# Adapter numbers read from DRAM into registers, and block 0's B and A sent on two queues behind the first piece of x

## The chip, the cores and the metric

The kernel runs on one core of a Trainium2 chip. The metric is the device time of that core in microseconds (us), and the figure for a kernel is the median of its runs.

## What is computed

x holds 8 sequences of 256 tokens with 1024 features, 2048 tokens in all. Each sequence has an adapter number between 3 and 7 that picks one of 8 pairs of low-rank matrices A (1024 x 16) and B (16 x 1024). The adapter's output goes through a feed-forward layer with 2752 hidden features whose inputs are rounded to FP8, and x is added at the end. In the reference, cut to what matters:

```python
def _L0_cond_ref(x, A, B, adapter_ids):
    B_sel = B[adapter_ids]
    A_sel = A[adapter_ids]
    Bx = jnp.einsum('bni,bri->bnr', x, B_sel)
    out = jnp.einsum('bnr,bor->bno', Bx, A_sel)
    return out * SCALING          # 1.0

def _fake_quant_fp8_linear(x, w_q, in_scale, w_scale):
    x_q = jnp.clip(x / in_scale, -_FP8_MAX, _FP8_MAX)
    x_dq = x_q.astype(jnp.float8_e4m3fn).astype(jnp.float32) * in_scale
    return jnp.einsum('bsh,ih->bsi', x_dq, w_q * w_scale)

gate_out = _fake_quant_fp8_linear(y, gate_w, gate_in_scale, gate_w_scale)
up_out = _fake_quant_fp8_linear(y, up_w, up_in_scale, up_w_scale)
hidden = jax.nn.silu(gate_out) * up_out
x = x + _fake_quant_fp8_linear(hidden, down_w, down_in_scale, down_w_scale)
```

## The kernel before

Everything is transposed: features lie on the 128 partitions, tokens along the rows. The 2048 tokens form four blocks t = 0 to 3 of 512, each of two sequences; the 1024 features form eight groups k of 128. The hidden features form 22 chunks c, 21 of 128 and a tail of 64. Weights lie in DRAM as float32, and TensorE reads the upper half of each word as bfloat16.

**The stages on TensorE (PE).** Every matmul goes through one helper at line 470, which holds PE to the order of the program. PE starts with 16 matmuls on a tile of zeros (`warm`, line 634), which need no data. Then it computes B times x for block 0 (`bx`, line 635, in the order of k, with 4 more matmuls on zeros after k = 3), 7 more matmuls on zeros, A times that (`c`, line 637), and then gate and up of chunk 0 for block 0 (`y`, line 638). ScalarE (ACT) and VectorE (DVE) round `c` to FP8 as `xg`. `turns=(2, 2, 2, 2)` at line 638 makes the first eight of chunk 0's sixteen matmuls read only the first half of its weights. Chunks 1 to 4 follow for block 0; in the middle of chunk 4 comes `bx` of block 1 (line 642), then the same five chunks for block 1, with B and A of blocks 2 and 3 among them, and so on; chunks 5 to 21 run over all four blocks; the down projection (`yd`) ends the kernel. After each gate and up, ACT applies Silu and DVE multiplies (lines 609 and 610).

**The loads, in the order of the program, lines 394 to 420.** x of block 0 comes in three pieces: k = 0 to 3 (1 MB), k = 4 to 6 (768 KB), k = 7 (256 KB). Below they are called x0, x4 and x7 after `load_x(0, 0)`, `load_x(0, 4)` and `load_x(0, 7)`. Gate and up weights of one chunk are 1 MB; chunk 0 comes in two halves (c0a, c0b), the others whole (c1 to c4). A load of B for one sequence is 68 KB in 128 rows (it also brings the six scales), one of A for block 0 or 1 is two transfers of 16 rows, 32 KB each. Nearly all are issued by SyncE's queue (SP); the adapter numbers and the B of sequence 0 are issued by ACT's.

**The adapter numbers.** Line 306 brings the eight numbers to SBUF (`ids_i`); `adapter_of` (line 363) loads one of them from SBUF into a register of the queue that asks, and checks its range. `load_b` (line 366), `load_a_two` (line 373) and line 420 use the register as an offset into DRAM. SP reads number 1 ahead of B of sequence 1 (line 396), number 0 between its A loads (line 402), and numbers 2 to 7 in a row (line 406), behind the loads of c0 to c4 and ahead of B and x of block 1.

**The limit on transfers in flight.** The framework gives the transfers of SP and ACT eight semaphores in turn, so a transfer is issued only when the one eight places before it has landed. SP carries out its queue in order; a wait at one transfer holds up all behind it.

**The tail of the down weights.** `wt` (line 656) is one transfer of 512 KB. The program has it near the end of the chunks; the framework's order puts it on SP's queue behind the A loads of blocks 2 and 3.

## Time and profile before

| | |
|---|---|
| median of 3 runs | 476.85 us (476.83 to 477.06) |
| time of the profiled execution | 477.12 us |
| its span, first to last instruction | 475.3 us |
| outside the span | 1.8 us |
| granted TensorE clock | 1.000 |
| PE busy | 469.8 us, 99% of the span, 2514 matmuls |
| ACT busy / DVE busy | 192.5 us / 105.6 us |
| read from HBM / written | 44.60 MB / 8.39 MB |
| waits of PE for a transfer, all before 17.3 us | 4, together 1.45 us |

All moments below are microseconds from the start of the span. A line such as `PE y L470 <- DMA w_gu<-w_gu` reads: the matmuls at line 470 that write `y` waited for the transfer from `w_gu` in DRAM to the tile `w_gu`. SPq and ACTq are the queues' own instructions: an issue of a transfer is a `DMA_DIRECT2D`, and the load of a register is a `TENSOR_LOAD`. "To landing" is the time from the start of an issue until all 16 parts of the transfer are down.

### The profile page before, as it was taken

What the parts mean: (1) busy time and instruction counts of PE and PEld (TensorE: products, weight loads), DVE (VectorE), ACT (ScalarE), POOL (GpSimd) and SP (SyncE); (2) the same over time, 40 slices, a digit from 0 to 9 for tenths busy, and PEclk for the clock granted to TensorE, in tenths of its full rate; (3) what the DMA queues carried; (4) which work ended last, traced back from release to release, by engine and by line L of the source; (5) the groups of instructions that cost most, each with busy time, mean ns of one, the idle gap of its engine ahead of it and who ended that gap; (6) DMA issues with size and microseconds to landing.
All of it is one profiled execution on the core that took longest, in us unless ns stands there. A gap on an engine that the chain in (4) does not pass through costs nothing.

```text
span 475.3 us, 6009 instructions
## 1 busy us (share of the span) xinstructions
PE 469.8 (99%) x2514; PEld 217.0 (46%) x2514; DVE 105.6 (22%) x163; ACT 192.5 (40%) x249; POOL 1.0 (0%) x7
## 2 busy tenths in 40 slices
PE   8999999999999999999999999999999999999997
PEld 4454544444444444444444444444444444444444
DVE  1333432121212222121212212132120121031031
ACT  1322447995556654533454554359212022021000
POOL 0000000000000000000000000000000000000000
PEclk9999999999999999999999999999999999999999
DMA  8995013422222112222211111123335255063031
GB/s 291 406 405 186 1 48 133 176 88 90 88 88 89 24 66 89 90 88 88 90 30 60 44 62 56 61 83 123 103 146 161 64 185 161 22 213 114 3 116 66
DMA packets 13780, 53.44 MB, mean 112 GB/s; under 512 B 1650, under 2 KB 2930, under 8 KB 10674
## 3 DMA queue, kind: packets, MB, share of 16 engines
q1 hardware_dynamic: 13600, 52.92, 32.1%
q8 instruction: 21, 0.34, 0.3%
q14 instruction: 13, 0.11, 0.1%
q10 hardware_dynamic: 146, 0.07, 0.0%
HBM read 44.60 MB, written 8.39 MB: 111 GB/s over the span
## 4 chain that ended last, share of the span: by engine, by line
PE 96%; DMA 3%; SPq 0%; issue 0%; DVE 0%
PE y L470 62%; PE yd L470 31%; DMA w_gu<-w_gu 2%; PE c L470 1%; PE bx L470 1%; DMA x<-x 1%; DMA ids_i<-ids 0%; SPq L363 0%; SPq L366 0%; DVE o L695 0%; PE count L470 0%
## 5 line engine op out<-in xcount | busy, mean ns | idle before, releaser
L470 PE MATMUL y<-xg,w_gu 128*128 128x512 fp8e4 x1376 | 298.4, 379 | 0.9 <-DMA w_gu<-w_gu 0.9
L470 PEld LDWEIGHTS <-w_gu 128*128 128x128 bf16 x1376 | 134.0, 98 | 163.8 <-DMA w_gu<-w_gu 1.8
L470 PE MATMUL yd<-hid,w_d 128*128 128x512 fp8e4 (+2 forms) x693 | 146.0, 373 | 0.0
L609 ACT ACTIVATE g<-y,gate_s 128x512 f32<-128x512 f32 (+1 forms) x88 | 59.8, 681 | 137.2 <-PE y L470 137.2
L610 DVE SCALAR_TENSOR_TENSOR hid<-y,up_by_down,g 128x512 fp8e4<-128x512 f32 x84 | 63.1, 751 | 220.3 <-PE y L470 162.2
L470 PEld LDWEIGHTS <-w_d 128*128 128x128 bf16 x693 | 66.6, 98 | 79.0 <-issue 1.7
L456 ACT ACTIVATE junk<-w_d 128x1408 bf16<-128x1408 uint16 (+1 forms) x16 | 21.2, 1324 | 88.4 <-DMA w_d<-w_d 88.3
L695 DVE SCALAR_TENSOR_TENSOR o<-yd,down_s,x 128x512 f32<-128x512 f32 x28 | 20.0, 748 | 107.4 <-PE yd L470 92.8
L456 ACT ACTIVATE junk<-w_gu 128x2048 bf16<-128x2048 uint16 (+1 forms) x22 | 41.0, 1863 | 0.0
L463 ACT ACTIVATE junk<-hid 128x2048 bf16<-128x2048 fp8e4 x21 | 40.0, 1905 | 0.4
L463 ACT ACTIVATE junk<-xg 128x2048 bf16<-128x2048 fp8e4 x8 | 15.3, 1909 | 0.3
L528 ACT ACTIVATE xg<-c,inv 128x512 fp8e4<-128x512 f32 x16 | 9.7, 688 | 8.6 <-PE c L470 8.6
L526 DVE TENSOR_SCALAR xg<-c,inv 128x512 fp8e4<-128x512 f32 x16 | 10.9, 744 | 2.8 <-PE c L470 2.8
L470 PE MATMUL warm<-zeros 128*128 128x512 bf16 (+1 forms) x27 | 6.5, 402 | 1.2 <-DVE zeros L309 1.2
L695 DVE SCALAR_TENSOR_TENSOR o<-yd,down_s,xg 128x512 f32<-128x512 f32 (+2 forms) x5 | 3.2, 644 | 12.3 <-PE yd L470 12.3
L516 ACT COPY bm<-bx 64x128 f32<-64x128 f32 x4 | 1.0, 262 | 9.7 <-PE bx L470 9.6
L470 PE MATMUL bx<-x,b 128*32 128x128 f32 x128 | 4.3, 276 | 0.6 <-DMA x<-x 0.6
L470 PEld LDWEIGHTS <-zeros 128*128 128x128 bf16 x27 | 2.6, 116 | 4.7 <-issue 3.0
L470 PE MATMUL c<-bm,a 32*128 32x128 f32 x128 | 4.3, 277 | 0.0
L456 ACT ACTIVATION_READ_ACCUMULATOR junk<-w_gu 128x1 f32 x22 | 4.2, 191 | 0.0
L470 PEld LDWEIGHTS c<-bm,a 32*128 32x128 f32 x128 | 3.9, 186 | 0.5 <-ACT bm L516 0.4
L470 PE MATMUL yd<-hid_tail,w_dt 64*128 64x512 bf16 (+1 forms) x32 | 4.1, 377 | 0.0
(47 smaller groups left out, 41.0 us busy)
## 6 DMA issues: line engine op xcount, KB each, us to landing
w_gu<-w_gu SPq DMA_DIRECT2D x20, 1024.0 KB, 4.8
outT<-o SPq DMA_DIRECT2D x31, 256.0 KB, 2.2
w_d<-w_d SPq DMA_DIRECT2D x8, 704.0 KB, 4.8
w_d<-w_d SPq DMA_DIRECT2D x8, 640.0 KB, 3.9
x<-x SPq DMA_DIRECT2D x2, 2048.0 KB, 11.1
x<-x SPq DMA_DIRECT2D x2, 1024.0 KB, 8.6
x<-x SPq DMA_DIRECT2D x2, 768.0 KB, 9.5
w_gu<-w_gu SPq DMA_DIRECT2D x3, 512.0 KB, 3.8
```

What stands on the lines that cost most here:

```text
L456: nc.scalar.activation(junk_like(w), low(w), AF.Copy, accum_out=lows[:rows, column : column + 1])
L463: nc.scalar.activation(junk_like(q), q, AF.Square, accum_out=squares[:rows, column : column + 1])
L470: tc.keep_in_program_order(nc.tensor.matmul(*args, **kwargs))
L516: copy(bm[64 * to : 64 * (to + 1), other], bx[half][64 * half : 64 * (half + 1)],)
L526: nc.vector.tensor_scalar(to, c, scale, None, ALU.mult, saturate=False)
L528: nc.scalar.activation(to, c, AF.Copy, scale=scale, saturate=False)
L609: nc.scalar.activation(g[rows], gates, AF.Silu, scale=gate_s[: gates.shape[0]])
L610: nc.vector.scalar_tensor_tensor(to, in0=ups, scalar=up_by_down[rows], in1=g[rows], op0=ALU.mult, op1=ALU.mult, saturate=False,)
L695: nc.vector.scalar_tensor_tensor(o, in0=y, scalar=down_s, in1=x, op0=ALU.mult, op1=ALU.add)
```

## The change

The adapter numbers are no longer brought to SBUF: `adapter_of` loads its register from the DRAM tensor itself. On SP, B and A of sequence 1 are issued right behind x0; B and A of sequence 0 are both issued on ACT's queue, which makes SP's second load of number 0 unnecessary. ACT's table load moves behind these issues. x4 and x7 follow on SP. The load of `wt` becomes two transfers.

```diff
-    ids_i = const.tile([1, NB], I32, name="ids_i")
-    nc.scalar.dma_start(out=ids_i, in_=ids)
-    nc.scalar.preload_act_table(AF.Silu)
...
         def adapter_of(batch, queue):
-            return queue.value_load(ids_i[0:1, batch : batch + 1], min_val=0, max_val=7)
+            return queue.value_load(ids[0:1, batch : batch + 1], min_val=0, max_val=7)
...
-        def load_a_two(t, j, adapter):
+        def load_a_two(t, j, adapter, queue=nc.sync):
             for g in range(2):
                 row = 32 * (2 * g + j) + R * j
-                nc.sync.dma_start(
+                queue.dma_start(
                     out=a_two[t][row : row + R],
                     in_=a8[bass.ds(adapter * 2 * R + g * R, R), :],
                 )
...
         load_x(0, 0)
-        load_b(b_two[0], 0, adapter_of(0, nc.scalar), nc.scalar)
-        second = adapter_of(1, nc.sync)
-        load_b(b_two[0], 1, second, nc.sync)
-
-
+        first, second = adapter_of(0, nc.scalar), adapter_of(1, nc.sync)
+        for j, adapter, queue in ((0, first, nc.scalar), (1, second, nc.sync)):
+            load_b(b_two[0], j, adapter, queue)
+        for j, adapter, queue in ((0, first, nc.scalar), (1, second, nc.sync)):
+            load_a_two(0, j, adapter, queue)
+        nc.scalar.preload_act_table(AF.Silu)
         load_x(0, 4)
-        load_a_two(0, 1, second)
-        load_a_two(0, 0, adapter_of(0, nc.sync))
         load_x(0, 7)
...
             if c == NI - 2:
-                nc.sync.dma_start(out=wt, in_=w_d_tail)
+                for ks in (slice(0, KS), slice(KS, NH)):
+                    nc.sync.dma_start(out=wt[:, ks], in_=w_d_tail[:, ks])
```

## The prediction, made before the changed kernel ran

> **What bounds the kernel now.** I read first the page's busy times (PE 469.8 of 475.3 us), then the list of PE's waits, then the chain that ended last, and then the first 18 us queue by queue, because nothing else of PE's time is idle. The chain, merged, in order of time (start, us, what):

> ```profile
> 0.74 1.18 DMA ids_i<-ids
> 1.94 0.46 SPq L363
> ...
> 2.92 0.37 SPq L366
> ...
> 3.33 4.97 DMA x<-x
> ...
> 8.32 8.85 DMA w_gu<-w_gu
> ...
> 17.21 13.12 PE y L470 x60
> ```

> The chain runs through numbers, register load, B's issue, x4 and c1, and from 17.21 us through matmuls alone. So what the change is worth is how far it moves 17.21. PE's timeline until then:

> ```profile
> 1.20 5.58 PE L470 MATMUL warm<-zeros 128*128 128x512 bf16 x16 [1.20 <-DVE zeros L309]
> 6.71 1.08 PE L470 MATMUL bx<-x,b 128*32 128x128 f32 x32
> 7.72 0.40 PE L470 MATMUL warm<-zeros 128*128 128x128 bf16 x4
> 8.34 0.86 PE L470 MATMUL bx<-x,b 128*32 128x128 f32 x24 [0.22 <-DMA x<-x]
> 9.59 0.43 PE L470 MATMUL bx<-x,b 128*32 128x128 f32 x8 [0.38 <-DMA x<-x]
> ...
> 14.70 1.90 PE L470 MATMUL y<-xg,w_gu 128*128 128x512 fp8e4 x8 [0.23 <-DMA w_gu<-w_gu]
> 17.21 13.12 PE L470 MATMUL y<-xg,w_gu 128*128 128x512 fp8e4 x60 [0.62 <-DMA w_gu<-w_gu]
> ```

> Two things are to be seen. `bx` starts at 6.71 because the 16 matmuls on zeros end there; B had landed by 6.25 and x0 by 5.74, so bringing B sooner moves nothing. And four waits, 0.22 + 0.38 + 0.23 + 0.62 = 1.45 us, for x4, x7, c0b and c1, are all that can be gained: 0.3%. SP's queue shows why these land when they do:

> ```profile
> 0.75 0.38 SPq L381 DMA_DIRECT2D x<-x  x1
> 2.92 0.37 SPq L366 DMA_DIRECT2D b<-b  x1
> 3.33 0.45 SPq L381 DMA_DIRECT2D x<-x  x1
> 4.00 2.58 SPq L373 DMA_DIRECT2D a<-a  x4
> 6.62 0.42 SPq L381 DMA_DIRECT2D x<-x  x1
> 7.09 2.99 SPq L391 DMA_DIRECT2D w_gu<-w_gu  x6
> 13.70 1.58 SPq L366 DMA_DIRECT2D b<-b  x2
> 15.33 2.19 SPq L381 DMA_DIRECT2D x<-x  x3
> ```

> and the rate of the first 12 us, in 40 slices of 0.3 us, the hole:

> ```profile
> GB/s 0 0 0 0 0 109 109 246 82 164 437 437 437 437 410 437 249 358 449 439 389 471 410 430 294 212 89 130 389 451 389 382 396 355 273 314 341 396 396 300
> ```

> From 7.2 to 8.4 us (294, 212, 89, 130) 0.22 MB moved where 0.5 MB could have: at 420 GB/s 0.69 us is lost. The 2.58 us of A's four issues (with the second load of number 0 among them) kept SP from x7 until 6.62, and its first packets came some 1.4 us later; all that SP had queued before (x0, both Bs, x4) was through at 7.3. Past the hole the rate is full until x of block 1 is in.

> [...]B of sequence 0 on ACT (issued 2.88) and of sequence 1 on SP (2.92) landed together, at 6.06 and 6.25. The prices of a register load from DRAM, which the trace doesn't show, [...] I write L for it[...]: the six loads of line 406 meet full DMA traffic.

> **Part by part.**
> - *The numbers' transfer goes, the load gets dearer (SP).* Before: x0's issue ends at 1.13, wait for the numbers until 1.94, load 0.46, 0.52 us of range check and address, B at 2.92. After: load from 1.16 to 2.46, B at 2.98. Nothing gained or lost at L = 1.3; each 0.1 us of L moves it 0.1. On ACT the load starts at 0.75 instead of 1.94, B of sequence 0 at 2.6 instead of 2.88. B must land by 6.71; between x0's packets it needs until some 6.4.
> - *A ahead of x4.* Two issues on SP with their address work: before, 0.22 from the end of the previous issue to the first A, then 0.58 to the second and 0.33 for it. So B 2.98 to 3.35, A 3.57 and 4.15 to 4.48, x4 at 4.52 instead of 3.33. Its packets can start some 1.4 us later, at 5.9; x0, B and now A (0.131 MB, 0.32 us at 410 GB/s) keep the engines until 5.6 + 0.3 = 5.9. No hole, but no slack: above L = 1.3 x4 itself opens one. x4 lands 0.32 later, at 8.62.
> - *x7 and c0 sooner.* SP would be free for x7 at 5.0, but x7 becomes the ninth transfer and waits for the first, x0 (5.74, with more packets among its own some 6.06). Issued at 6.1 it has packets at 7.5; x4's last are out at 7.5 + 0.32 = 7.8. c0a follows at 6.56 (waits for B, landed), c0b 7.0, c1 7.5. The hole closes, less what is left of the tightness: of 0.69 I take 0.6 for everything behind it. x7 lands at 8.95 instead of 9.55, c0b at 14.05 instead of 14.65, c1 at 16.57 instead of 17.17. (The last of c0b's 16 parts is 2.4 us behind the twelfth, and c1's likewise. I leave this lag as it is.)
> - *PE's sum.* `bx` of k = 4 to 6 from 8.62 (wait 0.50, before 0.22) for 0.86 to 9.49; x7 is there: saves the 0.38; `bx` ends 0.1 sooner, and so does everything up to `y` at 12.48 (before 12.58). Its first eight matmuls end at 14.36 (12.48 + 1.88), c0b is there: no wait; the next eight end at 16.26; c1 at 16.57, start at 16.6. 17.21 - 16.6 = 0.6 us gained. Were c1 earlier still, PE would be the bound at 16.26: at most 0.95 us.
> - *After that.* c2 was 1.0 us early (landed 19.64, needed 17.21 + 16 x 0.216 = 20.67) and moves with c1. No wait follows.
> - *Six loads from DRAM in a row on SP.* Before, a load with its check took 0.57, from 10.13 to 13.53. After they start at c4's end, 9.4 (c2 to c4 at 0.47 apart), and take 6 x (L + 0.3) = 9.6, until 19.0; then two Bs and x of block 1 at 20.0. That is 4.7 us later than 15.33, and hidden: the transfers queued ahead keep the engines until some 21.4, when nine of c4's 16 parts are down (22.1 to 22.4 before, less 0.6). Without this cover it costs; see the rivals.
> - *ACT's table load, 1.28 us,* behind four instructions: from some 4.2 to 5.4. ACT's next work is the copy of `bx` at 10.11. Nothing.
> - *`wt` in two:* one more issue (0.42) on SP at 36.7, ahead of loads that wait 30 us for a buffer. Nothing. It also brings the count of transfers back, so that the eight semaphores pair as before from there on.

> Sum: 477.12 - 0.6 = 476.5 for the profiled execution; it stands 0.27 above the median, so 476.25 for the median.

> **The rivals.**
> 1. *The hole only moves.* L near 1.8 in the first load delays x4 by 0.5; a hole of 0.5 us opens ahead of x4, the one behind it closes, and the gain is 0.1: 476.75. For it: no slack at 5.9. Against: a single load with little traffic.
> 2. *PE runs up to its own bound.* If x4 comes no later than before and the lagging parts of c0b and c1 catch up, the gain is 0.95 to 1.3: 475.8. For it: twelve of c0b's parts were down by 12.3. Against: the lag lasts through c1, c2, c3.
> 3. *The six loads starve the engines.* With L = 2.3 they end at 9.4 + 6 x 2.6 = 25.0, x of block 1 is issued at 26.0 and 26.5, its first seven groups (1.84 MB) begin at 27.4, take 4.5 us and land at 32.4[...]. `bx` of block 1 needs k = 4 at 31.27 - 0.6 = 30.67 (1.0 us after its start): 1.7 us of stall, net +1.1: 477.95. It decides from L = 2.0 on, where the stall begins, breaks even at 2.1, and each further 0.1 costs 0.6. [...]
> 4. *The load isn't from DRAM, or B and A are put elsewhere by the framework:* then nothing moves, 476.85. Little speaks for it.

> **How the numbers follow.** Forecast 52%, rival 1 and 4 together 16%, rival 2 10%, rival 3 22%. The measurement can tell about 0.2%, 0.95 us, from no change. The forecast and rivals 1 and 4 lie within it but for a few points at the forecast's upper edge (faster 3); rival 2 is faster by it, all but 1; rival 3 is slower by it in 18 of 22 (L above 2.3), the rest between. Faster 0.12, same 0.70, slower 0.18. Range 475.8 (rival 2) to 478.3 (rival 3 to L = 2.36; some 12% lie beyond it, and 5% below the range).

> **What would show it.** The load at line 363 in its mean time, first and later ones apart; x4's issue near 4.5 and x7's near 6.1, held by x0; the rate from 7.2 to 8.4 at 400; the four waits of PE as 0.5, 0, 0, 0.3; `y` of chunk 1 at 16.6; no wait of `bx` of block 1 for x. I am wrong if a load takes over 2 us, if x4 comes after 6, or if the lag of c0b's last parts changes.

## The result, and the profile after

The changed kernel takes 483.55 us (median of 4 runs, 482.74 to 484.26) against 476.85 us for the kernel before (476.83 to 477.06): a ratio of 1.0139, with a 95% interval of 1.0121 to 1.0157, or 6.7 us more. The profiled execution took 484.26 us (before 477.12), its span 482.4 us (before 475.3), and its mean granted clock is 0.996 (before 1.000). So 7.1 us of span have to be found. PE's timeline of the changed kernel shows where (start us, us, engine, line, operation, and in brackets the idle time before with what ended it):

```profile
7.03 1.08 PE L468 MATMUL bx<-x,b 128*32 128x128 f32 x32
...
10.81 1.08 PE L468 MATMUL bx<-x,b 128*32 128x128 f32 x32 [2.37 <-DMA x<-x]
...
18.22 13.12 PE L468 MATMUL y<-xg,w_gu 128*128 128x512 fp8e4 x60 [0.16 <-DMA w_gu<-w_gu]
34.77 1.08 PE L468 MATMUL bx<-x,b 128*32 128x128 f32 x32 [3.42 <-issue]
36.73 1.93 PE L468 MATMUL bx<-x,b 128*32 128x128 f32 x32 [0.88 <-DMA x<-x]
38.59 1.70 PE L468 MATMUL y<-xg,w_gu 128*128 128x512 fp8e4 x4
...
42.30 12.26 PE L468 MATMUL y<-xg,w_gu 128*128 128x512 fp8e4 x56
```

The same view of the kernel before, at `bx` of block 1 and at the first `y` behind `c`:

```profile
30.27 1.95 PE L470 MATMUL bx<-x,b 128*32 128x128 f32 x64
...
35.19 12.26 PE L470 MATMUL y<-xg,w_gu 128*128 128x512 fp8e4 x56
```

The four short waits of before have become one of 2.37 us for x4 and one of 0.16 us: chunk 1 starts at 18.22 instead of 17.21, 1.01 us later. Two new waits stand at `bx` of block 1. It starts at 34.77 where before it started at 30.27: another 3.49 us. (The 3.42 is put down to "issue", but x of block 1 landed at 34.68, 0.09 us ahead of the start.) From that `bx` to the next `y` behind `c` the changed kernel needs 7.53 us, until 42.30, the kernel before 4.92: another 2.61 us. 1.01 + 3.49 + 2.61 = 7.11.

Of the 2.61 us, 0.88 is the wait for x's second piece. The rest is the clock, which the view by windows shows (window, us, busy us of PE, weight load, DVE, ACT and POOL with their counts, granted clock, share of the DMA engines' time, GB/s):

```profile
24.00:28.00 4.00, 4.00 (x21) 1.82 (x19) 0.75 (x1) 0.99 (x2) 0.00 (x0) 1.00 0.03 10
31.00:36.00 5.00, 1.43 (x34) 0.84 (x32) 0.00 (x0) 0.21 (x1) 0.00 (x0) 1.00 0.95 373
36.60:40.00 3.40, 3.27 (x36) 1.81 (x36) 0.57 (x2) 0.52 (x2) 0.00 (x0) 0.50 1.05 400
40.00:45.00 5.00, 5.00 (x79) 3.24 (x78) 3.48 (x5) 2.42 (x4) 0.00 (x0) 1.00 0.97 398
```

From 36.6 to 40 us PE had half its clock: 3.41 us by the clock's record, 36.56 to 39.98, so 1.7 us lost. 0.5 x 3.41 / 482.4 = 0.0035 agrees with the mean clock of 0.996. And from 24 to 28 us the DMA engines had nothing to do (10 GB/s): they ran dry before x of block 1 was asked for.

SP's queue tells why. The chain that ended last, in its part that lies on SP (start us, us, what; L360 is `adapter_of`, L378 x):

```profile
1.18 1.86 SPq L360
...
3.14 1.10 SPq L360
...
10.42 4.19 SPq L360
14.72 1.03 SPq L360
...
16.05 3.39 SPq L360
19.53 0.89 SPq L360
...
26.61 0.83 SPq L360
27.54 0.46 SPq L360
...
29.39 0.43 SPq L378
29.86 6.82 DMA x<-x
```

Before, the chain was on PE from 17.21 us on; now it stays on SP until 29.8. Each number takes two loads, one behind the other, and their sources by name show what the first is for (times in ns: shortest, median, longest):

```profile
L360 SPq TENSOR_LOAD <-ids_ptr x7: 831/1733/4191, 1.2 to 26.6; - x7
L360 SPq TENSOR_LOAD <-ids x7: 459/459/1096, 3.1 to 27.5; - x7
```

First the address of the tensor is read (`ids_ptr`), then the number at that address. SP's issues follow from it:

```profile
4.74 0.37 SPq L363 DMA_DIRECT2D b<-b  x1
5.32 0.91 SPq L370 DMA_DIRECT2D a<-a  x2
6.27 0.90 SPq L378 DMA_DIRECT2D x<-x  x2
7.21 3.16 SPq L388 DMA_DIRECT2D w_gu<-w_gu  x6
28.45 0.89 SPq L363 DMA_DIRECT2D b<-b  x2
29.39 1.39 SPq L378 DMA_DIRECT2D x<-x  x3
```

x4 goes out at 6.27 (before 3.33), x of block 1 at 29.39 (before 15.33). The six loads in a row last from 10.42 to 28.29, 17.9 us (before 3.4).

### The profile page after: what moved, and what is told of

Read it like the earlier page. It is cut to its first block, busy times and chain, and to the rows that moved or that the text cites. A ratio compares the mean times of both kernels' runs of the same rounds, so it can differ in the third digit from the quotient of the medians.

```text
span 482.4 us, 6021 instructions
## 1 busy us (share of the span) xinstructions
PE 471.5 (98%) x2514; PEld 217.7 (45%) x2514; DVE 105.5 (22%) x163; ACT 192.4 (40%) x249; POOL 1.0 (0%) x7
## 4 chain that ended last, share of the span: by engine, by line
PE 92%; SPq 6%; DMA 1%; issue 1%; DVE 0%
PE y L468 58%; PE yd L468 31%; SPq L360 4%; DMA x<-x 1%; PE c L468 1%; PE bx L468 1%; SPq L388 1%; SPq L378 0%; SPq L363 0%; SPq L370 0%; DVE o L694 0%; PE count L468 0%
## 5 line engine op out<-in xcount | busy, mean ns | idle before, releaser
L468 PEld LDWEIGHTS bx<-x,b 128*32 128x32 f32 x128 | 3.8, 124 | 8.1 <-issue 4.3
L694 DVE SCALAR_TENSOR_TENSOR o<-yd,down_s,xg 128x512 f32<-128x512 f32 (+2 forms) x5 | 3.2, 644 | 12.3 <-PE yd L468 12.3
L514 DVE COPY bm<-bx 64x128 f32<-64x128 f32 x4 | 1.1, 283 | 14.6 <-PE bx L468 14.5
## 6 DMA issues: line engine op xcount, KB each, us to landing
x<-x SPq DMA_DIRECT2D x2, 2048.0 KB, 11.7
```

The costliest lines, as they stand in the source:

```text
L468: tc.keep_in_program_order(nc.tensor.matmul(*args, **kwargs))
L514: copy(bm[64 * to : 64 * (to + 1), other], bx[half][64 * half : 64 * (half + 1)],)
L694: nc.vector.scalar_tensor_tensor(o, in0=y, scalar=down_s, in1=x, op0=ALU.mult, op1=ALU.add)
```

## The experiments

In the expectations T is the theory that the time of the loads from DRAM is the loss; each names what stands against it, above all that the new order, with x4 behind A, costs time by itself. Differences in us are the ratio's excess times 476.6. Each kernel is "after" or "before" with the edit shown.

**Numbers from SBUF, the rest as changed (`e1`).**

```diff
+    ids_i = const.tile([1, NB], I32, name="ids_i")
+    nc.scalar.dma_start(out=ids_i, in_=ids)
...
-            return queue.value_load(ids[0:1, batch : batch + 1], min_val=0, max_val=7)
+            return queue.value_load(ids_i[0:1, batch : batch + 1], min_val=0, max_val=7)
```

> The changed kernel with one part undone: the numbers come through SBUF again, so its new order of B, A and x4 stands alone. Theory T (the register loads from DRAM cost all of it: two dependent reads each, one on SP ahead of x4, six ahead of x of block 1): x4 is issued near 4.5 us, x7 near 6.1, the hole before 8.4 us closes, chunk 1 of block 0 starts near 16.6 instead of 17.21; 476.0 to 476.8 us. Rival R (A ahead of x4, under eight semaphores, is what holds x4 up): x4 lands after 10 us, chunk 1 at 18.2; about 477.9 us.

Measured: 478.46 us, ratio 1.0053 (1.0038 to 1.0068), +2.5 us. T was too low, and R's 477.9 was the nearer: x4 reached PE at 9.88, and chunk 1 started at 17.27. PE's last matmul ended at 472.51, as before (472.46), but the span ended at 476.3 instead of 475.3: the end of the program took 3.74 us behind PE instead of 2.88. This kernel issues one transfer more than the kernel before. The eight semaphores go round in turn, so the last store got another one, and SP's final waits, one after the other, asked for it first, with seven more behind (474.54 to 475.38); before, it was asked for last. So e1 tells the new order and this tail (the time behind PE's last matmul) together; `f1` parts them.

**The old order with numbers from DRAM (`e2`).** The reverse: "before" with the two lines of `ids_i` out and `ids_i[` as `ids[`.

> The kernel before with one part done alone: the numbers from DRAM, its old order of transfers. T: the load on SP ends near 4.3 us instead of 2.4, so x4 is issued near 5.1; the second load of number 0, between the As, puts 2 us more ahead of x7 and chunk 0; the six loads take some 18 us and x of block 1 is issued near 33; 485.5 to 489 us. R: the loads themselves take little from the end, the order did it; at most 479 us.

Measured: 487.75 us, 1.0237 (1.0218 to 1.0256), +11.3 us: T held. The loads cost more in the old order than in the new one. In its trace SP reads number 0 once more in the midst of the traffic, and x of block 1 goes out at 32.53 (in the changed kernel 29.39). The two issues of x4 and x7 on SP show it, and between them stands that second read, 6.75 to 9.08:

```profile
5.14 0.43 SPq L379 DMA_DIRECT2D x<-x  x1
10.44 0.42 SPq L379 DMA_DIRECT2D x<-x  x1
```

PE waited 1.72 us for x4, 2.58 for x7, and at `bx` of block 1 2.90 and 0.58, with half clock twice (mean clock 0.989).

**Only the first two numbers, or only the six later ones, from DRAM (`e3`, `e4`).** e1 with

```diff
-        def adapter_of(batch, queue):
+        def adapter_of(batch, queue, src=ids):
...
-            return queue.value_load(ids[0:1, batch : batch + 1], min_val=0, max_val=7)
+            return queue.value_load(src[0:1, batch : batch + 1], min_val=0, max_val=7)
```

and `ids_i` given to the six later ones (e3) or to the first two (e4).

> The changed kernel with only the first two numbers (one load on SP, one on ACT) from DRAM, the six later ones from SBUF. T: x4 lands near 10.8 us and chunk 1 of block 0 starts near 18.2 as in the changed kernel, no wait at block 1's x; 476.85 + 1.0 = 477.6 to 478.1 us. R: the same place is late, but for the order, so that this run and the one with all numbers from SBUF have the same time.

> The changed kernel with only the six later numbers from DRAM, the first two from SBUF. T: the six loads begin near 9.4 us and take some 18; x of block 1 is issued near 28.5; PE waits some 4 us for B and x of block 1, then runs for 3.4 us at half the clock[...]; 482 to 483.5 us. R: under 478 us.

Measured: e3 479.94 us, 1.0078 (1.0065 to 1.0091), 1.2 us above e1 by the ratios, with intervals that touch. The traces show the place: PE's wait for x4 was 2.55 us (e1 1.95) and chunk 1 started at 18.64 (e1 17.27). T named the place rightly; its time was too low, since e3 has e1's tail too (3.70 us behind PE). e4 483.24 us, 1.0129 (1.0107 to 1.0152), 3.6 us above e1, within what T expected. Its six loads lasted from 8.96 to 26.7. The waits of e4 for x (all of them in us, their number, the longest):

```profile
PE bx L470 <- DMA x<-x: 4.8, 3, 3.3
```

3.29 us of it lies at `bx` of block 1, and half clock follows there too (mean clock 0.992). So both groups of loads cost, the six the larger and the surer part.

**The six loads done twice (`g4`).** "After" with the line `adapters = [...]` twice: the dose doubled.

> The changed kernel with the six loads done twice in a row. T (all that SP has behind the loads is late by their sum, and by then the transfers ahead have run out, so each costs its full price on the path): six more pairs at the undisturbed 1.67 us, 10.0 us more; x of block 1 is issued near 39.4; the kernel before plus 16 to 18 us. Rival (only the slow first loads matter, the rest hides): the kernel before plus 7 to 9 us.

Measured: 495.0 us, 1.0385 (1.0366 to 1.0403), +18.4 us, a little over T. The six extra pairs fall into the time when the engines are dry and take 0.83 + 0.46 us, 1.67 with the range check, as any pair there; x of block 1 is issued at 40.22, and PE waits for it:

```profile
PE bx L469 <- DMA x<-x: 16.7, 3, 13.8
```

Six times 1.67 is 10.0 us, x goes out 10.8 us later than in the changed kernel, and by the ratios the time grew by 11.7 us. Past the point where the cover ends, what SP spends on numbers is paid in full.

**Two numbers at a time (`f3`).** "After" with the six loads spread: two ahead of B and x of block 1, two behind each x of blocks 2 and 3.

```diff
-        adapters = [adapter_of(2 + q, nc.sync) for q in range(6)]
+        adapters = [adapter_of(2 + q, nc.sync) for q in range(2)]
...
         for t in (2, 3):
             load_x(t, 0)
+            adapters += [adapter_of(2 * t + q, nc.sync) for q in range(2)]
```

> The changed kernel with the six loads of numbers from DRAM spread: two ahead of B and x of block 1, two behind x of block 2, two behind x of block 3. T (what is queued on SP behind the six loads is what is late): the two loads end near 20 us, x of block 1 is issued near 21 instead of 29.4 and lands near 30, so PE waits for it by under 1 us; the later four may hold B of blocks 2 and 3 a little; the kernel before plus 1 to 3.5 us, at least 3 us under the changed kernel. Rival (the loads cost wherever they are, six times a fixed time on the path): no less than the changed kernel, the kernel before plus 6 us or more.

Measured: 479.26 us, 1.005 (1.0035 to 1.0065), +2.4 us where the changed kernel has +6.6: T held. The cover, the transfers queued ahead that keep the DMA engines at work while SP reads numbers, is restored, as SP's issues, PE's timeline and the window that was empty before (10 GB/s) show:

```profile
19.10 0.89 SPq L363 DMA_DIRECT2D b<-b  x2
20.03 1.38 SPq L378 DMA_DIRECT2D x<-x  x3
```

```profile
16.16 16.56 PE L469 MATMUL y<-xg,w_gu 128*128 128x512 fp8e4 x76
32.65 1.96 PE L469 MATMUL bx<-x,b 128*32 128x128 f32 x64
```

```profile
24.00:28.00 4.00, 4.00 (x20) 1.78 (x19) 0.83 (x2) 0.69 (x1) 0.00 (x0) 1.00 1.02 411
```

x of block 1 goes out at 20.03, the very time that the prediction had taken for it, and then `bx` follows `y` directly. What stays is the first two numbers: a wait of 2.76 us for x4 and half clock from 11.5 to 14.92.

**The new order alone, count of transfers as before (`f1`).** e1 with `wt` in one transfer again.

> The new order with the numbers from SBUF again, and wt in one transfer, so that the count of transfers is that of the kernel before. In the run with wt in two, some 0.9 us of its 2.15 lay at the very end: the last store had the semaphore that SP waits for first, so seven more waits came behind it; in the kernel before it has the one waited for last. Theory T2 (the new order itself opens a cold hole ahead of x4, the tail is a matter of the count): the tail is back to that of before, and the kernel before plus 0.6 to 1.4 us remains. Rival (the tail has nothing to do with the count, the new order costs all): the kernel before plus 2.1 us, as with wt in two.

Measured: 477.35 us (22 runs, 476.73 to 479.25), 1.0023 (1.0014 to 1.0032), +1.1 us by the ratio. T2 held: the tail is that of before (2.9 us), and the new order is still no gain. x4 was issued at 4.45 (predicted 4.52) and x7 at 5.70, as soon as x0 had landed (predicted 6.1). PE's timeline of its profiled execution, its rate of the first 12 us in 40 slices of 0.3 us, and a window:

```profile
7.30 0.40 PE L470 MATMUL warm<-zeros 128*128 128x128 bf16 x4
10.07 1.18 PE L470 MATMUL bx<-x,b 128*32 128x128 f32 x32 [2.38 <-DMA x<-x]
```

```profile
GB/s 0 0 0 0 0 137 164 55 191 300 328 437 410 382 437 437 266 313 372 212 143 61 266 225 369 430 369 328 369 410 260 321 369 375 362 300 259 259 382 396
```

```profile
10.95:14.30 3.35, 3.35 (x55) 2.92 (x51) 0.67 (x3) 0.67 (x3) 0.00 (x0) 0.50 1.01 391
```

The hole has moved from 7.2–8.4 us to 5.7–7.2 us (212, 143, 61, 266, 225), now ahead of x4. x4's packets began on time, the first nine between 5.86 and 6.14, but these took 0.48 to 0.94 us each, where x4's first nine took 0.23 to 0.25 us in the kernel before and in g1, with the engines at work. In 15 of the 22 runs (476.7 to 477.8 us) the mean clock was 1.000; in 7, the profiled one among them (478.4 to 479.3 us), it was 0.996, which is what one stretch of half clock makes; in the profiled one it lies behind the gap. The 15 lie 0.5 us above the mean of the kernel before, the 7 lie 2.1 us above it, so about half of the 1.1 us is this clock.

**`wt` in two transfers, nothing else (`f2`).** "Before" with the last part of the diff.

```diff
-                nc.sync.dma_start(out=wt, in_=w_d_tail)
+                for ks in (slice(0, KS), slice(KS, NH)):
+                    nc.sync.dma_start(out=wt[:, ks], in_=w_d_tail[:, ks])
```

> The kernel before with the load of wt in two transfers and nothing else: one transfer more in all. T2: PE's work doesn't move, the tail behind the last store grows by the seven waits; the kernel before plus 0.7 to 1.0 us. Rival (the split is free): within 0.2 us of the kernel before.

Measured: 477.05 us (22 runs), 1.0007 (0.9998 to 1.0016). Inconclusive: the interval, -0.1 to +0.8 us, holds no change as well as the lower end of what T2 expected. Its trace has a tail of 3.3 us behind PE against 2.9, of the kind seen in e1; a tail 0.4 us longer fits the +0.3 us of the ratio.

**All of block 0's B and A on ACT (`f4`).** "Before" with SP issuing x0, x4, x7 and the weights at once, numbers from SBUF; the table load of line 307 moves behind ACT's issues in the program, and `load_a_two` takes the queue as in the change.

```diff
-        load_b(b_two[0], 0, adapter_of(0, nc.scalar), nc.scalar)
-        second = adapter_of(1, nc.sync)
-        load_b(b_two[0], 1, second, nc.sync)
+        first = adapter_of(0, nc.scalar)
+        load_b(b_two[0], 0, first, nc.scalar)
+        second = adapter_of(1, nc.scalar)
+        load_b(b_two[0], 1, second, nc.scalar)
         load_x(0, 4)
-        load_a_two(0, 1, second)
-        load_a_two(0, 0, adapter_of(0, nc.sync))
+        load_a_two(0, 0, first, nc.scalar)
+        load_a_two(0, 1, second, nc.scalar)
+        nc.scalar.preload_act_table(AF.Silu)
         load_x(0, 7)
```

> From the kernel before: SP issues x0, x4, x7 and the weights without waiting for a number; ACT reads numbers 0 and 1 from SBUF and issues both Bs and all four As of block 0. T2: x4's packets follow x0's without a hole, x7 and chunk 0 are queued by 7 us, the four waits of PE shrink by 0.5 to 1 us in all; the kernel before minus 0.3 to 1.0 us. Rival (the parts of c0b and c1 that land last set the time whatever the queue does): within 0.2 us of the kernel before.

Measured: 478.2 us, 1.0028 (1.0019 to 1.0037): both theories missed. x4 landed early, at 7.63, but now B was late. PE's timeline and ACT's issues of B:

```profile
8.52 1.57 PE L469 MATMUL bx<-x,b 128*32 128x128 f32 x32 [1.68 <-DMA b<-b]
```

```profile
2.91 1.49 ACTq L365 DMA_DIRECT2D b<-b  x2
```

The first B was issued at 2.91 and moved its first packets at 6.4, behind x4, which SP had issued at 1.18; it landed at 8.38. In this trace B, on ACT's queue, moved only when x4, queued earlier on SP, was nearly through (it landed at 7.63).

**A behind x4, on two queues, numbers from SBUF (`g1`).** This takes from the change only what had not hurt: SP's second load of number 0 goes, A of sequence 0 goes to ACT, but x4 stays ahead of A. (`load_a_two` takes the queue as in the change.)

```diff
         load_x(0, 0)
-        load_b(b_two[0], 0, adapter_of(0, nc.scalar), nc.scalar)
-        second = adapter_of(1, nc.sync)
+        first, second = adapter_of(0, nc.scalar), adapter_of(1, nc.sync)
+        load_b(b_two[0], 0, first, nc.scalar)
         load_b(b_two[0], 1, second, nc.sync)
         load_x(0, 4)
-        load_a_two(0, 1, second)
-        load_a_two(0, 0, adapter_of(0, nc.sync))
+        load_a_two(0, 0, first, nc.scalar)
+        load_a_two(0, 1, second)
         load_x(0, 7)
```

> From the kernel before, numbers from SBUF: A of sequence 0 goes on ACT's queue with its B, as in the change, but x4 stays ahead of both As; SP's second load of number 0 is gone. T2 (in the new order it is A ahead of x4 that lets the engines run dry and start cold): x4 lands by 8.6 us as before, x7 is issued at 5.75 (as soon as x0 has landed) instead of 6.62, the hole behind x4 shrinks; the kernel before minus 0.2 to 0.8 us, and at least 0.8 us under the new order with numbers from SBUF. Rival (two queues at once are what disturbs x4): x4 lands after 9.5, the kernel before plus 0.5 us or more.

Measured: 476.14 us (21 runs), 0.999 (0.9984 to 0.9997), 0.47 us below the kernel before and the only kernel here that beats it: T2 held. PE's timeline and the rate:

```profile
8.73 1.25 PE L468 MATMUL bx<-x,b 128*32 128x128 f32 x32 [0.53 <-DMA x<-x]
...
12.54 16.56 PE L468 MATMUL y<-xg,w_gu 128*128 128x512 fp8e4 x76
```

```profile
GB/s 0 0 0 0 0 137 218 27 109 300 437 437 437 382 437 410 244 406 467 331 300 423 348 369 403 342 335 246 348 437 410 410 382 328 355 382 423 410 410 423
```

One wait of 0.53 us is left of the four, no hole, and `y` runs unbroken from 12.54 through chunk 1 (15.99): the profiled span is 474.1 us. f1 and g1 differ in A's place against x4 (the table load stands elsewhere in the program but ran at 1.30 in both), and by the ratios in 0.0033, 1.6 us.

**x of block 0 in two pieces (`g2`).** g1 without `load_x(0, 7)`, the pieces k = 0 to 3 and 4 to 7, and `wt` in two. Its last residual of block 0 for k = 7 still reads the old layout, so that part of the output isn't the reference's.

> As the last kernel, and x of block 0 in two pieces, k = 0 to 3 and k = 4 to 7, so that no piece waits for the landing of x0 (wt in two keeps the count of transfers). T2: no hole at all before chunk 0; the second piece lands near 8.9 us, PE waits once for it, some 0.7 us, then not for chunk 0; the kernel before minus 0.3 to 1.0 us. Rival (the last parts of c0b and c1 set the time): within 0.2 us of the kernel before.

Measured: 476.59 us, 1.0004 (0.9997 to 1.0011): T2 missed, no gain left. The rival's number was right, but not its reason: `y` ran unbroken behind `bx`, and what PE waited for, 1.18 us, was the larger piece, which landed at 9.48; chunk 1 started at 16.61. In 4 of the 22 runs the mean clock was 0.996.

**Loads of numbers that nobody uses, on GpSimd (`g3`).** "Before" with

```diff
+        probe = [nc.gpsimd.value_load(ids[0:1, q % 8 : q % 8 + 1], min_val=0, max_val=7) for q in range(24)]
         load_x(0, 0)
```

> The kernel before with 24 numbers loaded from DRAM on GpSimd's queue, which has no work and no transfers; nothing uses them. It measures the load by itself. T3 (the load waits in DRAM traffic, whoever asks): a pair of dependent reads takes 2.5 to 5 us while the transfers run at full rate (to 36 us), 1.3 to 1.8 us after. T4 (it is SP's own queued transfers that hold SP's load up): a pair on GpSimd takes 1.3 to 1.8 us throughout. Both: the time of the kernel is that of before.

Measured: 476.73 us, one run; nothing waits for GpSimd. T3 held: the loads are slow while transfers flow, whoever asks; T4 fell. Where on their way the loads wait isn't shown. Loads of the address and of the number by source, first those between 5 and 30 us, then those between 39 and 62 us:

```profile
L394 POOLq TENSOR_LOAD <-ids_ptr x7: 1237/2143/3577, 3.7 to 26.2; - x7
L394 POOLq TENSOR_LOAD <-ids x7: 597/1024/1863, 6.0 to 28.7; - x7
```

```profile
L394 POOLq TENSOR_LOAD <-ids_ptr x12: 873/878/1081, 39.6 to 58.9; - x12
L394 POOLq TENSOR_LOAD <-ids x13: 484/484/617, 38.4 to 59.9; - x13
```

From 5 to 30 us, with 384 GB/s flowing on the mean, the medians are 2.14 + 1.02 us; from 39 to 62 us, with 43 GB/s, 0.88 + 0.48.

## Why the prediction was wrong, by its steps

The forecast was 476.25 us and the range ended at 478.3; the time was 483.55. The mechanism was the one of rival 3, at a size that the range left out.

- **What bounds the kernel: right.** Chunk 1's start, and past it only x of block 1, decide. All of the 7.1 us lies at these two places. (One slip of the reading changes nothing: B of sequence 0 was on ACT's queue, not SP's, and x4's last packets ended at 7.64, not 7.3.)
- **L, the price of a load: the step that failed.** L stands in the prediction for the time of one register load from DRAM. The trace of before shows none (its nine loads from SBUF took 0.26 to 0.46 us); the 1.3 us behind the forecast was the author's assumption. It isn't a single load: an address, then a number. So the 1.3 us taken for one load was the time of two, 0.83 + 0.46 = 1.29 us, and that only from 23 us on, as the engines ran dry; SP's first pair took 2.96, ACT's 2.57, and the first three of the six 5.22, 4.28 and 2.19. In traffic the load of the address alone took 2.14 us (g3, median on GpSimd). What the forecast lacked was the second load and the traffic; its range of times ended at L = 2.36, and the mean of the six was 17.9 / 6 - 0.3 = 2.68.
- **Numbers' transfer goes, B at 2.98: wrong, 4.74.** This is L again: 1.66 us more than 1.3 (2.96 - 1.3), and B came 1.76 later.
- **A ahead of x4, "no hole, but no slack", x4 down at 8.62: failed by itself too.** f1 kept the issue times (x4 4.45, predicted 4.52), and x4's first packets began when computed (5.86, predicted 5.9), but not at full rate: 61 to 266 GB/s until 7.2, and PE got x4 1.4 us later than computed (10.07). g1, with x4 ahead of A, has no such hole. In the changed kernel, where x4 was issued at 6.27, the thin stretch is 5.1 to 8.1 us (125 GB/s) and the landing 10.77. This was rival 1, which put it down to a longer L; in f1 it came without. The price is +1.1 us by f1 where that rival had 0.1 of gain left.
- **x7 held by x0, c0 behind it: right in f1**, and somewhat sooner than predicted (x7 5.70 for 6.1, c0 6.10 for 6.56), but without effect, since PE then stood at x4.
- **Gain of 0.6 at chunk 1: not there.** 17.21 became 18.22. But the gain existed: g1, with no load from DRAM and A behind x4, has chunk 1 at 15.99 in its trace, and by the ratio it gains 0.5 us.
- **The six loads: the largest term.** 17.9 us instead of 9.6, x of block 1 at 29.39 instead of 20.0. f3 shows that the cover was judged rightly: issued at 20.03, x is in time. Rival 3 counts 0.5 us from x's last packet to its landing (the trace of before has 0.37 for x0, 5.37 to 5.74, and 0.66 for x4, 7.64 to 8.30). Its own rule, 1.1 us at L = 2.3 and 0.6 for each further 0.1, gives 1.1 + 0.6 x 3.8 = 3.4 us at 2.68. Add the 0.6 us of gain that this rule had taken off and that did not come, the 1.0 us for x4 and the 1.7 us of half clock: 6.7 us, what the medians differ by (the profiled executions by 7.1). It is a sum of rounded parts and was put together afterwards.
- **Half clock: not foreseen.** 1.7 us behind the wait at `bx` of block 1. No line of before shows one (though 2 of 43 later runs of that kernel have a mean clock of 0.996, at 478.0 us), and the prediction priced a wait at its length alone.
- **ACT's table load: right in its effect.** It ran from 5.75 to 7.03 (predicted 4.2 to 5.4); ACT's next work was at 11.98.
- **`wt` in two as repair of the count: right in the changed kernel** (its tail is 2.9 us, as before; e1 without this balance has 1.4 us more than f1, 0.9 of it seen in the tail); what it costs alone stays open (f2).

The difference between the changed kernel and f1 (1.0139 against 1.0023, 5.5 us) is what the loads from DRAM cost, apart from `wt`, which f1 has in one transfer (f2 bounds that at 0.8 us); the new order costs the other 1.1 us.

## What to carry to other kernels

A register load from DRAM was here two loads, one behind the other, and their price went with the traffic at their moment, from 1.3 to 5.2 us for the pair: price it at the busiest stretch that it meets, and multiply by the number of loads that stand in a row ahead of the next big transfer. A queue that issues ahead of need has a cover; when a step lengthens, compute when the engines run dry, since from there the delay is paid in full (in g4 x of block 1 went out 10.8 us later, and the time grew by 11.7). Small transfers that are needed later go behind the large one that is needed next, even where they seem to fit into a gap; here that was worth 1.6 us.

## What the runs showed of the hardware that was not expected

```profile
29.74:33.15 3.41, 1.61 (x8) 0.52 (x6) 0.00 (x0) 0.69 (x1) 0.00 (x0) 1.00 0.86 274
33.15:36.56 3.41, 1.08 (x32) 0.84 (x32) 0.00 (x0) 0.00 (x0) 0.00 (x0) 1.00 1.05 412
```

```profile
7.26:10.67 3.41, 1.66 (x46) 1.02 (x34) 0.00 (x0) 0.00 (x0) 0.00 (x0) 1.00 0.49 193
```

So a stretch with a third or half of its time at work was followed by half clock. Waits of 2.38 (f1), 2.76 (f3), 3.29 (e4) and 3.42 us (the changed kernel) had it behind them, and it cost another 1.7 us in the changed kernel; those for x4 of 2.37 us in the changed kernel and 2.55 us in e3 had none.

- **A transfer on ACT's queue moved among SP's only in part.** In twelve of the traces B of sequence 0, issued on ACT at 2.87 to 4.02, first moved at 4.76 to 5.06, just before x0, on SP's queue, was through (5.19 to 5.37). In f4 B, issued at 2.91, let most of x4 pass too, which SP had issued at 1.18, and first moved at 6.41. In g1 the A on ACT's queue, issued at 3.47, moved from 5.72 on among x4's packets (5.36 to 7.97), which SP had issued at 3.33. What decides wasn't followed.
- **After a pause the first packets were slow, but not always alike.** x4's first nine took 0.48 to 0.94 us in f1 and 0.49 to 0.97 in g4, but 0.23 to 0.59 in the changed kernel and 0.27 to 0.69 in f3; without a pause ahead of them (the kernel before, g1) 0.23 to 0.25. The cause wasn't followed.
- **The count of transfers moved the end.** One transfer more (e1) changed which semaphore the last store had and with it how many waits SP still had to go through: 0.9 us of span with PE's end unchanged. The four traces with one transfer more (e1, e3, e4, f2) have 3.3 to 3.7 us behind PE's end, the ten others 2.88 to 2.94.
